# Fewer pieces of the second image's statistics in the fill, and a load step of its own

## Chip, cores, metric

One NeuronCore of a Trainium2 chip runs the whole program. The metric is the device time of one execution in microseconds, given as the median of several runs. The engines are called PE (matmul), DVE (VectorE), ACT (ScalarE), POOL (GpSimd) and SP (the queue that issues most DMAs).

## What is computed

Two images of 512 channels and 64 x 64 pixels pass two layers in float32, each with a group norm ahead of it and a residual around it:

```
x = x + L0(groupnorm(x))   # deformable convolution: 3x3 depthwise features -> offsets and masks,
                           # bilinear sampling of x @ in_w in 16 groups of 9 points, @ out_w
x = x + L1(groupnorm(x))   # attention over 4096 pixels, value and output product,
                           # batch norm over both images, relu
```

The group norm has 32 groups of 16 channels; the mean and variance are over a group's channels and all pixels of one image:

```python
def _gn(v, G=32, eps=1e-5):
    g = v.reshape(B_, G, C_ // G, H_, W_)
    m = jnp.mean(g, axis=(2, 3, 4), keepdims=True)
    s = jnp.var(g, axis=(2, 3, 4), keepdims=True)
    return ((g - m) / jnp.sqrt(s + eps)).reshape(v.shape)
```

Layer 0's group norm of the second image is what the change is about.

## The kernel before

Each image lies as 4 blocks (`kb`) of 128 channels by 4096 pixels, and is cut into 8 chunks of 8 rows (512 pixels). Layer 0 handles 16 chunks (`NSEQ`), eight of each image, as a software pipeline of generators. `project(i)` normalizes a chunk on ACT (L773, into `xn`), multiplies by `in_w` on PE (L783), copies the product to `xj` on ACT (L789), and writes it to a DRAM table (L791, SP). `features(i)` makes the depthwise convolution: the first tap of each channel block on ACT (L808), eight taps each on DVE (L814), the sums over blocks on POOL (`tot` L823 and L825, `sq` L841 and L843), the means on PE (`p_mean`, L830), then L835, L838, L847, L849, L850 and the Gelu L854. `weights(i)` makes the sampling weights: `po` on PE (L871), four adds on DVE (L876), Exp on ACT (L883), a run of DVE operations up to the nine products and sums L914 and L919, one ACT copy `at` (L922), and four transposes on PE (L930) that ACT copies to `awT` (L931). `sample(i)` spreads the weights (PE `pb` L959, ACT L964), contracts them with patches that SP has loaded (`fetch`, L943; PE `pa` L978, ACT L989), and multiplies by `out_w` (PE `py` L998, DVE L1003 and L1004).

All of it stands under `tc.manual_schedule()`: every engine runs its instructions in the order in which the Python code calls the generators. Each call of a generator emits the instructions up to its next `yield`. A fill, written out by hand (L1154 to L1212), brings the first three chunks to different stages; then the loop of L1213 runs one `period` for each chunk, with calls of the chains `y` and `m` (sample), `v` and `w` (weights), `f` and `g` (features) and `p` (project) interleaved by hand. The last two iterations have periods of their own. At the end of a period `w()` emits L922; at the start of the next, `y()` emits `py`, `v(4)` the four transposes, and `f(4)` four taps, followed by `y()` with L1003 and `f(9)` with nine taps.

The statistics of the second image have no place of their own. `image_stats(1)` is a generator called `later`, and `more()` advances it by one step. Its first step loads three pieces of 512 pixels (256 KB each) through ACT's DMA queue (L725) into three buffers, two in the tile `early` and one called `xraw`. Each further step takes one of 32 pieces: `refill()` loads the piece two ahead into the buffer that was read one step earlier, and `bn_stats` on DVE (L738) reads the oldest. After every eighth piece `bn_aggr` (L740) condenses a channel block. Six last steps close the group norm: the last L740; a small matmul on PE (L609); three DVE operations (L612 to L615); a second matmul (L618); one DVE operation and the square root on ACT (L621, L622); and the reciprocal, bias and two copies on DVE (L625 to L747).

In the fill `more()` is called once after `border()`, and twice in each of four turns around L876: one load step and eight pieces. A period calls it six times: after `v(4)`, after `f(4)`, after the nine and the seven taps with the following L876, ahead of the next-to-last `f()`, and in the third turn of its last loop. Periods for i = 0 to 4 thus have 30 calls. Ahead of the period for i = 5, `run(later)` at L1215 runs whatever steps are left, and then SP loads weights into the place of `early` (L1217). That period's `project(8)` is the first to use the second image's scale and bias.

Layer 1 (from L1233) works through attention for each image, mainly on PE.

## Time and profile before

| | us |
|---|---|
| median of 3 runs | 3643.39 |
| lowest and highest | 3637.86, 3644.47 |
| the profiled execution | 3641.34 |
| its span, first to last instruction | 3639.5 |
| PE busy in the span | 3406.3 (94%) |
| DVE busy | 2356.1 (65%) |
| ACT busy | 1305.9 (36%) |

The profile is of one execution, and all times in it count from the first instruction. Layer 0 fills about its first third. A line of the timeline gives the start, the duration, the engine, the line of the kernel, the operation with its tiles as out<-in, how many were merged, and in brackets how long the engine had stood idle and what ended that. A line of the chain gives the start, the duration and the work, in order of time, of those pieces of work that were each released by the one before.

| operation | us each |
|---|---|
| L738 `bn_stats` of one piece | 0.68 |
| L740 `bn_aggr` | 0.37 |
| L876 add | 0.59 |
| L814 tap (807 ns mean) | 0.81 |
| L922 copy | 2.94 |

### The profile page before, as it was taken

The page shows a single profiled execution, that of the slowest core. Times are in us where ns is not written, and L with a number is a line of the kernel's source. Part 1 is how long each engine was busy: PE and PEld are TensorE (multiplying, and loading weights), DVE is VectorE, ACT ScalarE, POOL GpSimd, SP SyncE. Part 2 cuts the span into 40 slices and gives each one's busy share as a digit, 9 for nine tenths or more (in the row PEclk, how much of TensorE's full clock was granted, in tenths as well). Part 3 has the DMA queues.
Part 4 walks back from the last instruction along what each step waited for, and adds up shares of the span by engine and source line. Part 5 has one row for each costly group of instructions (what it writes and reads, how often), then busy time and mean ns, then how long its engine had stood idle before and what let it go on. Part 6 is the DMA issues. An engine that isn't in the chain of part 4 may idle for free.

```text
span 3639.5 us, 38933 instructions
## 1 busy us (share of the span) xinstructions
PE 3406.3 (94%) x15155; PEld 2428.3 (67%) x15155; DVE 2356.1 (65%) x3549; ACT 1305.9 (36%) x1693; POOL 284.7 (8%) x190
## 2 busy tenths in 40 slices
PE   5789999999998999999999999999999999999990
PEld 2355555555555677777777777777777777777770
DVE  8899999999995674554555455476455545545544
ACT  2577778878876321111211111121111111111115
POOL 1121121121120110000000000031000000000000
PEclk9899999999999999999999999999999999999995
DMA  6334334334323444333433433444333343333359
GB/s 213 98 114 141 124 97 128 114 98 129 109 90 105 169 169 152 126 124 126 143 124 113 157 124 103 142 182 175 125 130 113 104 152 112 113 132 124 112 185 375
DMA packets 173942, 497.31 MB, mean 137 GB/s; under 512 B 21521, under 2 KB 55057, under 8 KB 164273
## 3 DMA queue, kind: packets, MB, share of 16 engines
q1 hardware_dynamic: 165360, 460.09, 37.4%
q10 hardware_dynamic: 8352, 34.61, 2.7%
q8 instruction: 121, 1.98, 0.2%
q14 instruction: 77, 0.62, 0.0%
q0 software_dynamic: 32, 0.00, 0.0%
HBM read 403.34 MB, written 91.29 MB: 136 GB/s over the span
## 4 chain that ended last, share of the span: by engine, by line
PE 77%; DVE 15%; DMA 4%; ACT 2%; issue 1%; POOL 1%; SPq 0%; ACTq 0%; DVEq 0%; POOLq 0%
PE acc L1497 42%; DVE conv L814 10%; PE pS L1342 7%; PE p L1540 6%; PE py L998 6%; PE pq L783 5%; PE pa L978 5%; PE pv L1382 3%; PE pk L1436 1%; DMA early<-in_x 1%; PE p_mean L830 1%; DMA v<-wv 1%; DVE o L876 1%; DMA in_w<-in_L_conv_in_w 1%; DMA out<-ct 0%
## 5 line engine op out<-in xcount | busy, mean ns | idle before, releaser
L1497 PE MATMUL acc<-e,v 128*128 128x256 f32 x3072 | 768.2, 386 | 0.0
L1346 ACT ACTIVATE e<-pS 128x1024 f32<-128x1024 f32 x256 | 262.1, 1024 | 1386.8 <-PE pS L1342 1318.4
L1497 PE MATMUL acc<-tt,v 128*128 128x256 f32 x3072 | 748.2, 380 | 0.6 <-DMA v<-wv 0.6
L1497 PEld LDWEIGHTS acc<-e,v 128*128 128x128 f32 x3072 | 566.5, 190 | 233.2 <-issue 165.4
L1497 PEld LDWEIGHTS acc<-tt,v 128*128 128x128 f32 x3072 | 582.4, 190 | 91.3 <-issue 10.6
L1349 DVE TENSOR_TENSOR t<-e 128x256 f32<-128x256 f32 x256 | 108.8, 425 | 761.6 <-ACT e L1346 761.6
L814 DVE SCALAR_TENSOR_TENSOR conv<-xn,L_conv_dw_w_sb,conv 128x504 f32<-128x504 f32 (+1 forms) x512 | 409.3, 807 | 35.4 <-ACT conv L808 21.5
L1359 DVE TENSOR_TENSOR tot<-tot,e 128x512 f32<-128x512 f32 x480 | 330.0, 687 | 8.3
L978 PEld LDWEIGHTS pa<-bt,patch 96*128 96x128 f32 x2048 | 250.9, 197 | 63.0 <-issue 34.7
L1342 PE MATMUL pS<-q,kq 64*128 64x512 f32 x1024 | 289.0, 641 | 0.0
L978 PE MATMUL pa<-bt,patch 96*128 96x128 f32 x2048 | 255.0, 281 | 12.9 <-ACT dT L989 5.8
L964 ACT COPY bt<-pb 96x1024 f32<-96x1024 f32 x124 | 234.9, 2008 | 57.0 <-PE pb L959 54.0
L783 PE MATMUL pq<-in_w,xn 128*128 128x512 f32 x512 | 239.0, 610 | 6.6 <-DVE o L876 4.5
L998 PE MATMUL py<-dT,L_conv_out_w_sb 128*128 128x512 f32 x512 | 234.3, 602 | 0.0
L1540 PE MATMUL p<-t,v 128*128 128x256 f32 x1024 | 231.6, 382 | 1.9 <-DMA v<-wv 1.9
L1540 PEld LDWEIGHTS p<-t,v 128*128 128x128 f32 x1024 | 192.0, 190 | 48.9 <-issue 21.2
L871 PE MATMUL po<-om_w_pg,feat 128*128 128x432 f32 x512 | 203.0, 542 | 2.5 <-ACT feat L854 2.5
L989 ACT COPY dT<-pa 32x256 f32<-32x256 f32 x496 | 179.5, 362 | 62.1 <-PE pa L978 52.8
L998 PEld LDWEIGHTS py<-dT,L_conv_out_w_sb 128*128 128x128 f32 x512 | 97.2, 193 | 117.3 <-issue 113.1
L783 PEld LDWEIGHTS pq<-in_w,xn 128*128 128x128 f32 x512 | 94.7, 195 | 113.6 <-issue 97.6
L871 PEld LDWEIGHTS po<-om_w_pg,feat 128*128 128x128 f32 x512 | 93.0, 191 | 93.8 <-issue 88.1
L1342 PEld LDWEIGHTS pS<-q,kq 64*128 64x128 f32 x1024 | 77.1, 184 | 84.9 <-issue 84.9
(210 smaller groups left out, 3710.1 us busy)
## 6 DMA issues: line engine op xcount, KB each, us to landing
v<-wv SPq DMA_DIRECT2D x252, 768.0 KB
patch<-xt SPq DMA_DIRECT2D x256, 192.0 KB
v<-wv SPq DMA_DIRECT2D x256, 128.0 KB
wv<-v SPq DMA_DIRECT2D x32, 896.0 KB
xt<-xj SPq DMA_DIRECT2D x128, 128.0 KB
res<-in_x SPq DMA_DIRECT2D x64, 256.0 KB
wx<-res SPq DMA_DIRECT2D x64, 256.0 KB
xq<-wx SPq DMA_DIRECT2D x16, 1024.0 KB
```

The costliest lines, as they stand in the source:

```text
L783: nc.tensor.matmul(pq, xn[:, kb, 1 + 2 * t : 3 + 2 * t, :].rearrange("p r c -> p (r c)"), in_w[:, kb, :], start=(kb == 0), stop=(kb == KB ...
L814: nc.vector.scalar_tensor_tensor(dst, src, wt, dst, ALU.mult, ALU.add)
L871: nc.tensor.matmul(po[:, : 3 * GP], f[:, kb, t * P : (t + 1) * P], om_w[:, kb].rearrange("p a k g -> p (a k g)"), start=(kb == 0), stop=(k ...
L964: copy(bt[:SN].rearrange("s g q d -> s d (g q)")[:, d0 : d0 + 4, :], pb[:SN])
L978: nc.tensor.matmul(pa[:, p], xp[:SN, p, cb * P : (cb + 1) * P], bt[:SN, 4 * cb : 4 * cb + 4, PX * s + p, :], start=True, stop=True,)
L989: copy(dst, src)
L998: nc.tensor.matmul(py, out_w[:, kb, cb * P : (cb + 1) * P], dT[:, kb, :], start=(kb == 0), stop=(kb == KB - 1))
L1342: nc.tensor.matmul(pS[:, h, :], kq[r, 2 * (kp // 4) + h, c0 : c0 + P], qs[qb][r, :], start=True, stop=True)
L1346: nc.scalar.activation(e.rearrange("p a q -> p (a q)"), pS.rearrange("p h q -> p (h q)"), AF.Exp)
L1359: nc.vector.tensor_add(tots[qb], tots[qb], e2[:, h, :])
L1497: nc.tensor.matmul(acc[j][:, cb * HQ : (cb + 1) * HQ], v[:, j, cb * P : (cb + 1) * P], ops[j], start=(kp + cb == 0), stop=(kp + cb == NPAI ...
L1540: nc.tensor.matmul(p7[:, cb * HQ : (cb + 1) * HQ], v7[:, cb * P : (cb + 1) * P], t3, start=(k + cb == 0), stop=(k + cb == NPAIR + 2),)
```

## The change

Three edits in the order of the calls and one in the generator. The call after `border()` is removed. In the four turns around L876 there is one call in each of the first three instead of two in all four. One call is added at the end of the fill, ahead of the loop. In `image_stats`, pieces ahead of the fourth of channel block 0 don't refill; at the fourth, `refill()` loads three pieces and the step ends there with a `yield`, so that the piece itself is taken at the next call; from the fifth on, it is as before.

```diff
                     if n == 0:
                         t = img[kb][:, h * CH : (h + 1) * CH]
                     else:
-                        refill()
+                        if (kb, h) == (0, 3):
+                            refill()
+                            yield
+                        elif (kb, h) > (0, 3):
+                            refill()
                         t = ahead.popleft()
                     nc.vector.bn_stats(st[:, h, :], t)
                     yield
...
             border()
-            more()
             p1(3)
...
             for t in range(4):
                 v()
-                more()
-                more()
+                if t < 3:
+                    more()
                 v()
...
             v()
+            more()
             for i in range(NSEQ):
                 if i == NCH - 3:
                     run(later)
```

## The prediction

> **What bounds the kernel now.** I read the page first: the slices, then the chain that ended last, then the chain in order of time and each engine's timeline around the calls that move.

> ```profile
> PE   5789999999998999999999999999999999999990
> ...
> DVE  8899999999995674554555455476455545545544
> ...
> PE 77%; DVE 15%; DMA 4%; ACT 2%; issue 1%; POOL 1%; SPq 0%; ACTq 0%; DVEq 0%; POOLq 0%
> ```

> From slice 14 on PE alone is the bound, and nothing of the change lies there. In the first dozen slices both PE and DVE are nearly full; only the time of each wait tells which decides. The DVE timeline of the fill (start, duration, idle before and its releaser):

> ```profile
> 100.94 1.28 DVE L738 BATCH_NORM_STATS2 gn_st<-early 128x6 f32<-128x512 f32 x2
> ...
> 108.96 0.69 DVE L738 BATCH_NORM_STATS2 gn_st<-early 128x6 f32<-128x512 f32 x1 [5.64 <-DMA early<-in_x]
> ...
> 111.45 0.69 DVE L738 BATCH_NORM_STATS2 gn_st<-early 128x6 f32<-128x512 f32 x1 [1.29 <-DMA early<-in_x]
> ...
> 118.75 0.69 DVE L738 BATCH_NORM_STATS2 gn_st<-early 128x6 f32<-128x512 f32 x1 [4.54 <-DMA early<-in_x]
> ...
> 121.07 2.27 DVE L835 TENSOR_TENSOR conv<-conv,p_mean 128x2048 f32<-128x2048 f32 x1
> ```

> Eight pieces take DVE from 100.94 to 121.07, and 12.84 us of it is waiting for loads (with 0.86 and 0.51 not shown). The chain passes through two of them:

> ```profile
> 104.12 7.31 DMA early<-in_x
> 112.61 7.32 DMA early<-in_x
> 225.35 6.36 DMA early<-in_x
> ```

> From 121 to 151 DVE is busy 29.24 of 30 us, so what is won before 121 moves the whole fill. Further on I call the loop's iterations P0 to P15 and date each by the start of its nine taps (L814): 155.69, 223.66, 295.13, 364.74, 436.35, 504.48, 572.29. P1 to P3, which hold six pieces each, last 71.47, 69.61 and 71.61 us; P4, where the six calls are the group norm's steps, 68.13; P5, with no call, 67.81. The chain in each: DVE's taps, POOL's `tot`, p_mean, then PE.

> The end of P4 on ScalarE and DVE:

> ```profile
> 497.73 2.93 ACT L808 ACTIVATE conv<-xn,L_conv_dw_b_sb,L_conv_dw_w_sb 128x512 f32<-128x512 f32 x4
> ...
> 501.16 2.94 ACT L922 COPY at<-aw 128x1600 f32<-128x1600 f32 x1
> 504.85 2.05 ACT L931 COPY awT<-p_tr 128x512 f32<-128x512 f32 x4 [0.75 <-PE p_tr L930]
> ```
> ```profile
> 498.57 3.09 DVE L814 SCALAR_TENSOR_TENSOR conv<-xn,L_conv_dw_w_sb,conv 128x504 f32<-128x504 f32 x4 [1.43 <-ACT conv L808]
> 503.08 0.75 DVE L1003 SCALAR_TENSOR_TENSOR res<-py,L_conv_out_b_sb,res 128x512 f32<-128x512 f32 x1 [1.42 <-PE py L998]
> ```

> L922 is the last instruction of P4's `weights`, so whatever `run(later)` issues on ScalarE stands behind it, and on DVE ahead of the taps of 498.57.

> [...] the trace has 1.28 us, and I use that. [...] In the fill the trace shows 6.4 to 7.3, beside the patch loads. [...] idle 1.33 us before p_mean leaves it at 1.13 us; after 5.52 us it takes 2.08, and the matmuls behind are slow too.

> **Counting the calls.** `image_stats(1)` has 40 steps after the change: one load step, 32 pieces, one added step at piece 3 that only loads, six that close the group norm. The calls before P5 are four in the fill and 30 in P0 to P4. The first (t = 0) loads pieces 0 to 2; the second and third take pieces 0 and 1; the last takes piece 2. The next loads therefore come with P0's first call, not at the fill's end. P0's other five calls take pieces 3 to 7, P1 to P3 six each, P4 pieces 26 to 31. All six closing steps fall into `run(later)` ahead of P5.

> **1. The fill, -8.6 us.** The removed call after `border()` had three loads on ScalarE's queue at 52.69, 0.33 to 0.46 us each, in a gap; nothing there gets faster. They are now issued when ScalarE has passed L808, near 102.0, where the first refill goes out today (102.07). The sixteen patch loads on SP (97.87 to 116.9) run then, as now. With today's 6.9 us (102.07 to 108.96) piece 0 starts near 109.0. Today's next load went out 2 us later and landed at 111.45; three without a wait on DVE can follow at 0.4 us, so piece 1 is there between 109.7 and 111.4. Piece 1 and two adds (L876) are 1.7 us: L835 starts at 111.4 to 113.1 instead of 121.07, a gain of 8.0 to 9.7. I take 8.6. p_mean is ready at 105.8 and would stop it there at best. Bounds: 11 if the loads take 5.4 us, 2 if they queue behind the patches. The L725 waits that hold ScalarE's Exp (L883) for 15.0 us vanish, which only keeps up with DVE. SP and POOL get no instruction more.

> **2. P0's first load, +6.0 us.** Let X be the end of the last L919, 151.10 now. ScalarE issues P0's first load at 157.65, X + 6.55, after L922 and the four L931. Today pieces 8 and 9 are long there and the nine taps start at X + 4.59. After the change DVE does piece 2 and four taps, stands at piece 3 from X + 3.8, and waits for a load that only goes out at X + 6.55. Patches are not running: the load of 157.65 was used at 163.07 without idle, so at most 5.4 us; two of three loads' packets had gone by 160.9. I take 3.4 [...]. Piece 3 then starts at X + 9.95, the nine taps at X + 10.6: 6.0 us later [...]. Everything behind on DVE waits with it; PE, ScalarE and POOL have slack to the next p_mean. ScalarE's next refill then waits for piece 3 at X + 10.6, ahead of a copy L964 that starts at X + 12.5 now: nothing.

> **3. P4 gets six pieces, +2.7 us.** The pieces of the first two calls fit into idle before L814 and L1003 (1.06 and 1.43). At the third, a load wait as in P1 to P3 (0.50, 0.61, 0.98) and 0.61, less three small group-norm operations of 0.47; at the fourth 0.61: together 1.3 to 1.7. PE's idle before p_mean goes from 1.64 to about 3.1, where P1 and P3 paid about 1.7 us for a cold clock and P2 did not. The mean of P1 to P3, 70.90, less 68.13 gives 2.8; I take 2.7 (1.3 to 3.5).

> **4. The chain ahead of P5, +7.8 us.** DVE runs bn_aggr (0.37) by 497.6; PE runs p1 only after pq, 499.45; DVE the three small ones, PE p2, DVE var, by about 502 (for image 0, p1 to var took 2.95 us). The root L622 stands behind L922, which ends at 504.10, and needs a table load: 504.10 + 1.28 + 0.29 = 505.7. DVE then does L625 to L747, 0.61, and starts the four taps at 506.3 instead of 498.57. Four taps, L1003 and L1004 follow without the 1.42 idle: nine taps at 510.7 instead of 504.48, +6.2. Behind them are queued all of P5's taps, so p_mean comes 6.2 late, after some 6 us of idle PE: +1.6 for the cold clock, as at P0 and P3. py is 1.5 to 2.6 late on PE, p_tr and L931 about 1: hidden under the 6.2. The `wkq` loads on SP wait for the last piece of `early`, near 494: nothing. Range 5.5 to 8.5.

> Sum: -8.6 + 6.0 + 2.7 + 7.8 = **+7.9 us**. The durations are of one execution, 3641.34 us with a span of 3639.5; it is 2.05 below the median of the three runs, 3643.39. The same difference on the median: 3651.3.

> **The rivals.**
> A. Not slower: the closing chain is hidden. Place: DVE's taps at 498.57; price 7.8. It decides if the root is done before 498.6, which needs the steps to end inside P4 or L622 to get ahead of L922. By the count and by L922's place it can't. Then +0.1: 3643.5.
> B. The fill's loads queue behind the patches. For: DVE still waited 4.54 us at 118.75, and the issues of 104.12 and 106.60 came about 2 us apart with nothing of DVE's pending. Then the gain is 2 and the sum +14.5: 3657.9.
> C. The loads do go out at the fill's end, as the change's name has it. Then step 2 is nought: +1.9, 3645.3. The count speaks against it.

> **How the numbers follow.** A measurement of this kernel can tell about 0.2%, 7.3 us, from no change. Forecast 0.68, its own range +4 to +11.5, of which 0.42 lies above 7.3; A 0.10; B 0.14; C 0.05; 0.03 for A and C together with the fill's best gain. Slower 0.56, same 0.41, faster 0.03. The range leaves out the ends of A and B: 3645 to 3657.

> **What would show it.** Right: L835 near 112; idle of about 6 us before the second-call piece of P0; P4 near 71 us; L622 after an ACT_TABLE_LOAD behind L922, and nine taps of P5 6 us late with a p_mean of about 2 us. Wrong: a root that stands in P4, no idle in P0, or L835 still near 118.

## The result and the profile after

| | before | after |
|---|---|---|
| median of 11 runs each | 3643.64 us | 3649.47 us |
| lowest to highest | 3637.86 to 3646.41 | 3646.22 to 3651.96 |
| the profiled execution | 3641.34 | 3647.23 |

The medians differ by 5.8 us. The ratio of the times is estimated as 1.0018, with a 95% interval of 1.0010 to 1.0027, which is 3.6 to 9.8 us: the changed kernel is slower. It was forecast as +7.9, between +1.6 and +13.6. Whether it passes 0.2% the interval does not decide. In the changed kernel the lines stand 4 further down (L738 is L742, L814 L818, L835 L839, L876 L880, L922 L926, L998 L1002). The slices look as before:

```profile
PE   5789989999998999999999999999999999999990
...
DVE  8899989999996674554554555476455545545544
...
PE 77%; DVE 15%; DMA 4%; ACT 2%; issue 1%; POOL 1%; SPq 0%; DVEq 0%; ACTq 0%; POOLq 0%
```

A change of 0.2% can't be read there. It can be read from events that both kernels have: the start of L835 in the fill, and the start of the nine taps of each period (the first L814 behind L1004; in P0, behind its second call), all from DVE's timelines. (For P6 the prediction has 572.29, from the chain; DVE's timeline has 572.21, so P5 took 67.73 us and not 67.81.)

| event | before | after | after less before | gained or lost since the row above |
|---|---|---|---|---|
| L835 of the fill | 121.07 | 112.28 | -8.79 | -8.79 |
| nine taps of P0 | 155.69 | 152.43 | -3.26 | +5.53 |
| nine taps of P4 | 436.35 | 434.18 | -2.17 | +1.09 |
| nine taps of P5 | 504.48 | 511.62 | +7.14 | +9.31 |
| nine taps of P6 | 572.21 | 581.15 | +8.94 | +1.80 |
| nine taps of P13 | 1046.22 | 1055.28 | +9.06 | +0.12 |
| end of the span | 3639.5 | 3645.4 | +5.9 | -3.2 |

DVE's timeline of the fill and of P0 after the change:

```profile
108.59 0.70 DVE L742 BATCH_NORM_STATS2 gn_st<-early 128x6 f32<-128x512 f32 x1 [7.15 <-DMA early<-in_x]
...
110.65 0.69 DVE L742 BATCH_NORM_STATS2 gn_st<-early 128x6 f32<-128x512 f32 x1 [0.86 <-DMA early<-in_x]
111.26 1.10 DVE L880 TENSOR_TENSOR o<-po,om_b_pg 128x432 f32<-128x432 f32 x2
112.28 2.28 DVE L839 TENSOR_TENSOR conv<-conv,p_mean 128x2048 f32<-128x2048 f32 x1
...
142.32 0.69 DVE L742 BATCH_NORM_STATS2 gn_st<-xraw 128x6 f32<-128x512 f32 x1
142.93 3.07 DVE L818 SCALAR_TENSOR_TENSOR conv<-xn,L_conv_dw_w_sb,conv 128x504 f32<-128x504 f32 x4
151.82 0.69 DVE L742 BATCH_NORM_STATS2 gn_st<-early 128x6 f32<-128x512 f32 x1 [5.82 <-DMA early<-in_x]
```

In the kernel before the same place of P0 shows no wait:

```profile
155.08 0.69 DVE L738 BATCH_NORM_STATS2 gn_st<-early 128x6 f32<-128x512 f32 x1
```

The 12.84 us of waits in the fill have become 8.01, and a wait of 5.82 is new in P0. The fourth piece is the one that pays: its load goes out with P0's first call, its bn_stats with the second. The chain in order of time says the same of the loads:

```profile
103.89 6.74 DMA early<-in_x
...
148.99 2.80 DMA early<-in_x
```

The end of P4, ScalarE first, then DVE:

```profile
502.19 2.92 ACT L926 COPY at<-aw 128x1600 f32<-128x1600 f32 x1
505.12 1.28 ACT L622 ACT_TABLE_LOAD   x1
506.42 0.30 ACT L622 ACTIVATE gn_var<-gn_var,eps 128x4 f32<-128x4 f32 x1
```
```profile
501.88 0.16 DVE L621 TENSOR_TENSOR gn_var<-gn_gm,gn_p 128x4 f32<-128x4 f32 x1 [0.54 <-PE gn_p L618]
506.75 0.18 DVE L625 RECIPROCAL gn_sc<-gn_var 128x4 f32<-128x4 f32 x1 [4.71 <-ACT gn_var L622]
...
507.24 3.08 DVE L818 SCALAR_TENSOR_TENSOR conv<-xn,L_conv_dw_w_sb,conv 128x504 f32<-128x504 f32 x4
```

DVE has the variance at 501.88 and gets the root at 506.75, because ScalarE copies `at` and loads a table first. All taps of P5 stand behind the reciprocal. PE waits for them; the first line is the kernel before:

```profile
530.44 1.13 PE L830 MATMUL p_mean<-tot,ones_c 128*128 128x512 f32 x2 [1.33 <-POOL tot L825]
```
```profile
537.58 2.08 PE L834 MATMUL p_mean<-tot,ones_c 128*128 128x512 f32 x2 [6.67 <-POOL tot L829]
539.45 4.48 PE L1002 MATMUL py<-dT,L_conv_out_w_sb 128*128 128x512 f32 x8
```

### The profile page after: what moved, and what is told of

It reads as the page before. It is cut to its first block, busy times and chain, and to the rows that moved or that the text cites. A ratio compares the mean times of both kernels' runs of the same rounds, so it can differ in the third digit from the quotient of the medians.

```text
span 3645.4 us, 38931 instructions
## 1 busy us (share of the span) xinstructions
PE 3409.0 (94%) x15155; PEld 2429.5 (67%) x15155; DVE 2357.5 (65%) x3549; ACT 1308.3 (36%) x1694; POOL 285.0 (8%) x190
## 4 chain that ended last, share of the span: by engine, by line
PE 77%; DVE 15%; DMA 4%; ACT 2%; issue 1%; POOL 1%; SPq 0%; DVEq 0%; ACTq 0%; POOLq 0%
PE acc L1501 42%; DVE conv L818 9%; PE pS L1346 7%; PE p L1544 7%; PE py L1002 5%; PE pq L787 4%; PE pa L982 4%; PE pv L1386 3%; PE pk L1440 1%; DMA early<-in_x 1%; PE p_mean L834 1%; DVE o L880 1%; DMA in_w<-in_L_conv_in_w 1%; ACT at L926 0%; DMA out<-ct 0%
## 5 line engine op out<-in xcount | busy, mean ns | idle before, releaser
L1501 PEld LDWEIGHTS acc<-tt,v 128*128 128x128 f32 x3072 | 582.4, 190 | 90.9 <-issue 10.6
L818 DVE SCALAR_TENSOR_TENSOR conv<-xn,L_conv_dw_w_sb,conv 128x504 f32<-128x504 f32 (+1 forms) x512 | 409.4, 808 | 34.4 <-ACT conv L812 20.5
L1002 PE MATMUL py<-dT,L_conv_out_w_sb 128*128 128x512 f32 x512 | 237.3, 608 | 0.0
L1002 PEld LDWEIGHTS py<-dT,L_conv_out_w_sb 128*128 128x128 f32 x512 | 98.5, 196 | 119.8 <-issue 115.3
```

The costliest lines, as they stand in the source:

```text
L818: nc.vector.scalar_tensor_tensor(dst, src, wt, dst, ALU.mult, ALU.add)
L1002: nc.tensor.matmul(py, out_w[:, kb, cb * P : (cb + 1) * P], dT[:, kb, :], start=(kb == 0), stop=(kb == KB - 1))
L1501: nc.tensor.matmul(acc[j][:, cb * HQ : (cb + 1) * HQ], v[:, j, cb * P : (cb + 1) * P], ops[j], start=(kp + cb == 0), stop=(kp + cb == NPAI ...
```

## The experiments

All were compared with the kernel before on the same chip; e1, e2, e3 and e5 shared one set of its runs (median 3641.79), e4, e6, e7 and e8 another (3642.28). The changed kernel was not run again beside them; where one is compared with it in time, both are taken as differences from their own runs of the kernel before, and the changed kernel stands at +5.8 us.

**e1: the closing chain alone, on the kernel before.**

```diff
-                period(y, v, m, w, f, g, Chain(project, i + 3), more)
+                period(y, v, m, w, f, g, Chain(project, i + 3), more if i < 4 else int)
```

> The kernel before, with its fill, and no calls of more() in P4, so that run(later) issues the six closing steps of the group norm ahead of P5 as after the change; nothing else is moved. Theory (the closing chain costs by its place): nine taps of P5 come 6.2 us later than before and P5 lasts 69.5 us for 67.7 (cold PE), P4's taps otherwise as before; in all +7.5 us against the kernel before. Rival (the loss in P4 and P5 is the six pieces and their loads, the chain is hidden): within 1 us of before.

Measured: 3648.03 us, ratio 1.0019 (1.0010 to 1.0029): 6.2 us over the kernel before, where 7.5 was expected. In the profile, from P4's nine taps to P5's it takes 73.79 us for 68.13, P5 69.65 for 67.73: together 7.6. DVE and ScalarE show the same picture as after the change:

```profile
508.80 0.18 DVE L625 RECIPROCAL gn_sc<-gn_var 128x4 f32<-128x4 f32 x1 [4.68 <-ACT gn_var L622]
```

So the place of the chain costs this with no piece in P4 at all, and the rival falls. The run shows something else. Up to P4 its program is that of the kernel before, yet P0 to P3 took 285.05 us for 280.67. In that stretch PE's granted clock was 0.95 for 0.97 in the mean: at half speed for 30.3 us in place of 18.6.

**e2: the closing chain spread over P5, on the changed kernel.** `gn[1]` is allocated ahead, so that `project(8)` can be built before it is written.

```diff
+        def close():
+            for _ in range(next(closing, 0)):
+                more()
...
-                    run(later)
+                    closing = iter((0, 2, 1))
+                    for _ in range(2):
+                        more()
...
             m()
+            late()
             p()
...
-                period(y, v, m, w, f, g, Chain(project, i + 3), more)
+                if i == NCH - 3:
+                    period(y, v, m, w, f, g, Chain(project, i + 3), close, more)
+                else:
+                    period(y, v, m, w, f, g, Chain(project, i + 3), more)
```

> The changed kernel, with the closing chain spread: bn_aggr and the first matmul ahead of P5, the three small operations and the second matmul at its second call, var and the root at its third, reciprocal, bias and copies just ahead of project(8). Theory: from P4's nine taps to P5's is 71 us for 77.4, P5 67.7 for 69.5; in all 8 us less than the changed kernel, 2 us less than before. Rival (the six pieces in P4 are the loss): stays within 2 us of the changed kernel. A second rival (the root pushes ScalarE's copies and so p_mean): half of the 8 us comes back.

Measured: 3640.90 us, ratio 0.9998 (0.9990 to 1.0007): 0.9 us under the kernel before and so 6.7 under the changed one, where 2 and 8 were expected. In the profiles, P4's nine taps to P5's: 71.19 us for 77.44; P5 67.80 for 69.53; together 7.98. On ScalarE the root now stands between two copies, with DVE far ahead of the need for it:

```profile
513.06 1.28 ACT L622 ACT_TABLE_LOAD   x1
514.35 0.30 ACT L622 ACTIVATE gn_var<-gn_var,eps 128x4 f32<-128x4 f32 x1
514.56 7.67 ACT L968 COPY bt<-pb 96x1024 f32<-96x1024 f32 x4
```

and p_mean follows after 0.60 us of idle:

```profile
531.87 1.12 PE L834 MATMUL p_mean<-tot,ones_c 128*128 128x512 f32 x2 [0.60 <-POOL tot L829]
```

The chain is free in this place. What is left of P4's loss, 71.19 - 68.13 = 3.1 us, is that of the six pieces. Both rivals fall.

**e3: the call after `border()` put back, on the changed kernel.**

```diff
             border()
+            more()
             p1(3)
```

> The changed kernel with the call after border() put back, so that pieces 0 to 2 are loaded 48 us ahead and the added load step runs at the fill's end, as the change's name has it; five closing steps stand ahead of P5. Theory: without a wait for a load L839 starts at 106, when p_mean is ready, for 112.3; P0 still waits, but about 2.6 us for 5.8; nine taps of P0 near 143.5 for 152.4, and in all 9 us less than the changed kernel, 3 us less than before. Rival (the fill is bound by ScalarE or PE once the wait is gone): L839 at 109 or later, or the gain is lost again before P0.

Measured: 3640.15 us, ratio 0.9997 (0.9989 to 1.0005): 1.6 us under the kernel before, where 3 was expected. L839 starts at 105.31, held only by p_mean:

```profile
105.31 2.29 DVE L839 TENSOR_TENSOR conv<-conv,p_mean 128x2048 f32<-128x2048 f32 x1 [0.25 <-PE p_mean L834]
```

So the wait for the first pieces was all that held the fill, 7.0 us of it. But P0's nine taps start at 144.57, not 143.5, since the load step at the fill's end still comes too late:

```profile
135.41 0.82 ACTq L725 DMA_DIRECT2D early<-in_x  x2
```
```profile
140.37 0.69 DVE L742 BATCH_NORM_STATS2 gn_st<-early 128x6 f32<-128x512 f32 x1 [4.92 <-DMA early<-in_x]
```

Issued at 135.41, used at 140.37: the load takes 5.0 us here, for 2.83 in P0 of the changed kernel, and P0's first call waits 4.92 us where the second had waited 5.82; 2.6 was expected. SP had issued its three loads of `raw` from 133.23 on, and between 135.4 and 140.4 its queue took 59% of the DMA engines' time; during the load of 148.99 in the changed kernel it moved nothing. That this is why the load took longer is not tested apart.

**e5: the patch loads of the fill behind four table writes, on the changed kernel.**

```diff
-            fetch(0, 0)
-            fetch(0, 1)
             f1()
             v()
             f1()
             v()
             p2(2)
             v(2)
             p2(2)
+            fetch(0, 0)
+            fetch(0, 1)
```

> The changed kernel with the two fetch calls of the fill behind the first four table writes of the third chunk, so that no patch load runs beside the loads of pieces 0 to 2. Theory (the patch loads on SP make these loads slow): the first piece starts about 4 us after its issue for 6.7, L839 at 108 for 112.3, in all 4 us less than the changed kernel. Rival (the time is that of three loads at once, whatever SP does): L839 stays at 112 and the time the same. If the patches come late for P0, its first pa waits and the gain is lost there.

Measured: 3642.90 us, ratio 1.0007 (0.9999 to 1.0015): 4.7 us under the changed kernel, where 4 was expected. The loads go out at 101.94 and the first piece is read at 105.04:

```profile
105.04 0.69 DVE L742 BATCH_NORM_STATS2 gn_st<-early 128x6 f32<-128x512 f32 x1 [3.57 <-DMA early<-in_x]
```

That is 3.1 us for 6.67 beside the patches; L839 starts at 107.78. What made the loads of the fill slow was the sixteen patch loads on SP's queue, which moved to 116.75, and P0 did not suffer.

**e4: e2 and e3 together** (`more()` once ahead of P5 instead of twice).

> Both repairs together: the call after border() back, as in e3, and the closing chain spread, as in e2. Theory (the two costs are separate): from P4's nine taps to P5's 71.2 us and P5 67.8, as in e2, behind a fill with L839 at 105.3, as in e3; 8 us less than e3, 9.6 us less than before. Rival (one hides the other): no more than 4 us less than e3.

Measured: 3634.71 us, ratio 0.9978 (0.9969 to 0.9987), 7.6 us under the kernel before, where 9.6 was expected. P5 is 67.81 as in e2, L839 at 105.07 as in e3. P4 is 71.92; p_mean there follows 3.25 us of idle and takes 2.08. Against the shared kernel before, e4 stands 5.9 us lower than e3, between the 8 of the theory and the 4 of the rival; in the profiles it is 77.29 + 69.37 - 71.92 - 67.81 = 6.9.

**e7: the load step ahead of `v(6)`, on e4.**

```diff
             p2()
+            more()
             v(6)
             next(products)
             run(output_bias())
             v()
-            more()
```

> e4 with the added load step called ahead of v(6) in the fill instead of at its end, so that pieces 3 to 5 are loaded while DVE still makes the sampling weights. Theory (P0's loss is a load issued too late): P0's first two pieces wait for nothing, its nine taps start 4.8 us after the end of the last L923 for 9.2 in e3, and the time is 4.4 us less than e4, 14 us less than before. Rival (P0's front is held by something else, ScalarE's copies or PE): P0 gets back less than 2 us of it.

Measured: 3630.12 us, ratio 0.9965 (0.9952 to 0.9977). The loads go out at 125.87, and P0 waits for nothing:

```profile
135.04 0.69 DVE L743 BATCH_NORM_STATS2 gn_st<-early 128x6 f32<-128x512 f32 x1
135.65 3.07 DVE L818 SCALAR_TENSOR_TENSOR conv<-xn,L_conv_dw_w_sb,conv 128x504 f32<-128x504 f32 x4
138.64 0.69 DVE L743 BATCH_NORM_STATS2 gn_st<-early 128x6 f32<-128x512 f32 x1
```

The nine taps start at 139.24, 4.2 us after the last L923 has ended. P0's loss was the time of that load's issue and nothing else. The time is 4.6 us less than e4's and 12.2 less than the kernel before, where 4.4 and 14 were expected.

**e6: PE kept busy ahead of P5's first p_mean, on the changed kernel.** The six added matmuls write what p_mean overwrites.

```diff
+                for _ in range(6 if warm else 0):
+                    nc.tensor.matmul(p, ones, in_w[:, 0, :], start=True, stop=True)
                 nc.tensor.matmul(p, ones, tot, start=True, stop=True)
...
-            mu = mean_over_c(tot)
+            mu = mean_over_c(tot, i == NCH - 1)
```

> The changed kernel with six matmuls of 128x512 on constants ahead of P5's first p_mean, into the same place, which p_mean then overwrites; they fill 5.2 us of the 6.67 us for which PE idles there. Theory (the 1.8 us by which P5 is longer is PE's clock after the idle): p_mean takes 1.1 us for 2.08 and py behind it 3.6 for 4.48, P5 lasts 67.8 for 69.53, in all 1.7 us less than the changed kernel. Rival (it is the late start itself, on DVE or ScalarE): P5 stays at 69.5.

```profile
533.43 5.32 PE L835 MATMUL p_mean<-in_w,ones_c 128*128 128x512 f32 x12
538.66 1.12 PE L836 MATMUL p_mean<-tot,ones_c 128*128 128x512 f32 x2
539.62 3.60 PE L1004 MATMUL py<-dT,L_conv_out_w_sb 128*128 128x512 f32 x8
```

p_mean takes 1.12 us for 2.08, py 3.60 for 4.48, and P5 67.75 us for 69.53. p_mean starts no earlier: 25.97 us behind the nine taps, for 25.96. The granted clock is 1.00 from 530 to 550 us. The time was 3647.21 us, ratio 1.0015 (1.0008 to 1.0021): in the total the 1.7 us can't be told from the changed kernel's 1.0018; in the stage they can.

**e8: the same with two matmuls in P1 to P4, on e7** (`3 <= i < NCH - 1`).

> e7 with two such matmuls (1.7 us) ahead of the first p_mean of P1 to P4, where PE idles about 3 us. Theory (whether such a gap leaves PE at half clock is what makes P1 to P3 differ by 2 us from one execution to the next): P1 to P4 are all near 69.6 us, in all 3 to 5 us less than e7. Rival (the differences come from the piece loads or the patches): no change beyond 1 us, or p_mean pushed back by the added matmuls.

Measured: 3622.87 us in five executions, ratio 0.9948 (0.9933 to 0.9962). P1 to P4 are 69.54, 70.05, 70.90 and 69.67 us; in e7 they were 71.57, 69.45, 73.72 and 71.96. In P1 the matmuls behind a p_mean of 1.12 are at full speed after a wait of 1.33:

```profile
233.20 1.88 PE L835 MATMUL p_mean<-in_w,ones_c 128*128 128x512 f32 x4
236.41 1.12 PE L836 MATMUL p_mean<-tot,ones_c 128*128 128x512 f32 x2 [1.33 <-POOL tot L829]
237.38 3.60 PE L1004 MATMUL py<-dT,L_conv_out_w_sb 128*128 128x512 f32 x8
```

The gain over e7, 7.3 us, is more than the 3 to 5 expected; the profiles show 6.5 in P1 to P4. All of that lies between the p_mean of `tot` and that of `sq`: 11.4 us or less in each of the four periods, where e7 has 13.1, 11.4, 14.5 and 13.1. So it is the clock and not the loads: granted to PE were 0.98, 1.00, 0.95 and 0.98 of full speed in P1 to P4 of e7, and 1.00, 1.00, 0.98 and 1.00 in e8. P3 is still 70.90: its third call waits 1.40 us for a load where P1's waits 0.56, and a `bn_aggr` of 0.36 stands behind it. This is the best of the kernels: 19.4 us, 0.5%, under the one before.

## Why the prediction was right, point by point

**The count of the calls held.** The added step loads in P0, not at the fill's end, and all six closing steps came behind P4.

**Step 1, forecast -8.6, was -8.79**, with L835 at 112.28 for 111.4 to 113.1. The estimate took the load's time from the refills beside the patches, 6.9 (102.07 to 108.96, of 6.4 to 7.3 for the first three); it was 6.67 (101.92 to 108.59). The second load went out 1.97 us behind the first, at 103.89, although no wait on DVE held it; that was within the bounds. Rival B has no case, but its reason was a real one: in e5, with the patch loads moved away, the load took 3.1 us for 6.67.

**Step 2, forecast +6.0, was +5.53.** Piece 3 was read 2.83 us after the issue at 148.99, for 3.4 assumed; that was the author's estimate, below the 5.4 us that the trace of the kernel before allowed (157.65 to 163.07).

**Step 3, forecast +2.7.** e2, which has the pieces in P4 and not the chain, puts it at 3.1. Both of its parts are in the changed kernel's trace: p_mean of P4 starts 27.84 us behind the nine taps for 26.36, and from there to the p_mean of `sq` PE takes 13.10 us for 11.40. The second part was luck: the gap ahead of p_mean in P4 was 3.09 us, and one of 3.07 in P2 of the same trace cost nothing: py behind it took 3.60 us at a granted clock of 1.00, and 5.03 in P4, where the clock was 0.50 from 462.70 to 466.12 (last section).

**Step 4, forecast +7.8.** Steps 3 and 4 together were 9.31 + 1.80 = 11.1 in this pair of profiles, for 10.5; e1 gives 5.66 + 1.92 for step 4, e2 7.98. The root starts 1.30 us after its table load does (505.12 to 506.42); the prediction had taken 1.28, the length of the table load in the trace of the kernel before (L883 at 119.84). The clock's part is shown by e6: with PE kept busy p_mean takes 1.12 us, and 2.08 after the idle of 6.67. Here it was hardly luck: of a gap of 6.67 us at least 3.3 fall into one of the clock record's stretches of 3.41 us, wherever they lie, an estimate from the figures of the last section, where half clock followed each of the eight gaps with 2.21 us or more in one stretch. Half clock came behind gaps of 2.69 to 3.26 us too.

The chain in order of time does not name this cause. In the changed kernel it reaches L1007 of P5 from a landing patch, though L1007 only followed its own engine's taps; what DVE waited for is in its timeline, 4.71 us for the root.

**Where the sum was off.** The four steps make 7.85 us in these profiles (-8.79 + 5.53 + 9.31 + 1.80), for 7.9. With the 1.09 of P0 to P3, where the change alters nothing, that is +8.94 at P6, against a total of +5.9 in the same profiles and 5.8 in the medians. The missing 3 us come after P13. From there to the end the kernel before took 2593.3 us in its profiled execution and the changed one 2590.1; the eight others, with nothing different in that part, took 2590.2 to 2593.7. So this is the scatter of executions, and it goes with PE's clock. Leaving out the last 83 us, which run at half clock in all ten (from 3556.91 us in the kernel before, from 3562.01 in the changed one), the clock was at half speed behind P13 for 23.9 us in the two executions that took longest there (the kernel before and e2), for 17.1 in the changed kernel, and for 17.1 or 20.5 in the others; 6.8 us at half speed are 3.4 us of PE's work. In P0 to P3 the same scatter ran the other way: the kernel before took 280.67 us in its profile and 285.05 in e1 with the same code. The sum was made against one execution and had no term for this. The interval of the ratio, 3.6 to 9.8 us, holds both the forecast and the measured median; whether more than chance lies between 7.9 and 5.8 it does not show. The prediction thought more than 7.3 us the likelier side, and the median lies on the other.

**The rivals.** A, a hidden chain, is excluded by e1 and is what e2 makes true by hand. C, loads at the fill's end, is what e3 builds; there the wait did not vanish, as I had written for C, but became 4.92 us. The end of the fill is too late for these loads as well: ScalarE gets there when DVE has just one instruction, L1147, ahead of P0's first call. Here the working of C was wrong: with nine taps 9.2 us after the last L923, for 4.6 before, it would have been +6.5 and not +1.9.

## What to carry to other kernels

When work is taken out of a generator that other code steps through, count the steps to the end: those that no call is left for run together at the place that closes it, and a short chain across three engines then holds everything behind its last link. What a step waits for decides its cost more than its own duration: a piece of 0.69 us cost 5.8 because its load was issued only when the engine already stood ready for it. Look for a place that the load's queue passes earlier, and see that no other queue's burst runs beside it: the load took 6.67 us beside the patches and 3.1 without them (e5).

## What was not expected of the hardware

- The length of a gap of about 3 us did not decide whether PE stood at half clock behind it. The gaps ahead of the p_mean of `tot`, from the PE timelines and clock records of the two traces:

  | trace, period | gap, us | most of it in one stretch, us | granted 0.50 | p_mean, us |
  |---|---|---|---|---|
  | before, P1 | 3.26 | 2.21 | 252.81 to 256.23 | 1.12 |
  | before, P2 | 3.13 | 1.84 | no | 1.13 |
  | before, P3 | 2.99 | 2.81 | 392.76 to 396.17 | 2.08 |
  | before, P4 | 1.64 | 1.64 | no | 1.12 |
  | before, P5 | 1.33 | 1.15 | no | 1.13 |
  | after, P1 | 2.69 | 1.92 | 247.66 to 254.49 | 2.08 |
  | after, P2 | 3.07 | 1.66 | no | 1.12 |
  | after, P3 | 2.91 | 2.91 | 391.02 to 394.44 | 1.74 |
  | after, P4 | 3.09 | 2.72 | 462.70 to 466.12 | 1.43 |
  | after, P5 | 6.67 | 3.41 | 534.38 to 541.21 | 2.08 |

  A stretch is 3.41 us: in both clock records the changes lie whole multiples of that apart (after the change 247.66, 391.02, 462.70 and 534.38 are 42, 21 and 21 of them apart), and how the stretches lie against the program differs between the two. Of all 23 gaps of over 1 us between 170 and 570 us in the two traces, each beginning at full clock, none of the 12 with at most 1.66 us in one stretch was followed by half clock, each of the eight with 2.21 us or more was, and two of the three between (1.73, 1.84, 1.92). These are counts of two executions. With what was left of these gaps at 1.44 us or less (e8), P1 to P4 were 6.5 us shorter in sum, and the time 7.3 us.
- Loads of 256 KB on ScalarE's queue took 2.8 to 3.1 us with no other queue moving data (P0 of the changed kernel, e5), 5.0 beside three loads of `raw` (e3), and 6.7 beside sixteen patch loads of 192 KB that SP's queue had issued.
